# A two-layer graph network: the second layer's attention, stepped in two parts inside the graph loop, with its weights made ahead of the loop and its last part two tiles at a time

## The chip, the core and the metric

The kernel runs on one core of a Trainium2 chip, in float32. A core has a TensorE (PE; its weight loads are listed as PEld), a VectorE (DVE), a ScalarE (ACT), a GpSimd (POOL) and a SyncE (SP) that issues transfers. Each engine executes its own instructions in program order; semaphores make one wait for another. What counts is the device time of the whole kernel in microseconds (us); lower is better.

## What is computed

Two layers over 3125 nodes with 256 features. Each layer adds three things to `x`: a graph part over 50000 edges (sorted by target), an attention, and a network of experts. The change is in the second layer's graph part and attention, which both read the normalised `xn`:

```python
# graph part: 4 heads, messages of 64 features, softmax over the edges of a target
h_fwd, h_rev = h @ W_forward.T, h @ W_reverse.T
messages = h_fwd[src] * direction[:, 0:1] + h_rev[src] * direction[:, 1:2]
scores = leaky_relu(einsum('ef,hf->eh', messages, attn_forward[0]), 0.2)
exp_scores = exp(scores - scores.max(axis=0, keepdims=True))
norm = exp_scores / (segment_sum(exp_scores, dst)[dst] + 1e-10)
out = [segment_sum(messages * norm[:, hd:hd + 1], dst) for hd in range(4)]
# attention without a softmax: 8 heads of 64
q, k, v = split(einsum('bnc,fc->bnf', x, Wqkv))
k, v = _inst_norm_lastdim(k), _inst_norm_lastdim(v)   # over the 64 of a head
dots = einsum('bhnd,bhne->bhde', k, v)
out = einsum('bhnd,bhde->bhne', q, dots) / n
return einsum('bnf,cf->bnc', out, Wout) + bout
...
x = x + _L1_gnn_ref(xn, ...) + _L1_mix_ref(xn[None], ...)[0]
x = x + _L1_ffn_ref(_layernorm(x), ...)[0]
```

## The kernel before

`x` lies in SBUF as 25 tiles of 125 nodes. Layer 0 comes first, then `layer1_mix`, then `layer1_ffn`. In `layer1_mix`, `experts_in` ends layer 0, normalises `x`, keeps the transposed result `xT` and writes a table `tab1` of both products and their scores (136 values a node) to DRAM. Then the stage that is changed begins.

**The graph loop.** The 50000 edges are 391 columns of 128, taken in 49 groups of up to 8. For a group `i`:

- `fetch` issues 8 indirect gathers on POOL (the helper at L51), one for each column, into a buffer `g` of which there are four. It runs three groups ahead.
- `messages` (L1223 to L1234): three VectorE instructions make the messages and so free `g`; L1227 the scores, L1232 their maximum over the columns, and PE transposes it into `psm` (L1234).
- `maximum` (L1241 to L1247): VectorE takes the running maximum of each head, PE spreads it over the partitions by two more transposes (L1247).
- `ones_of` (L1272): a 0/1 matrix `hot` for each node tile that the group can touch, two of them mostly. Groups that touch a tile with all 8 columns alternate with groups that touch one with few.
- `exponents` (L1252 to L1257): scores less the maximum, then two exponentials on ScalarE.
- one group later `weigh` (L1280) multiplies messages by the four weights into `v`, and `products` (L1288) sums them into node tiles by matmuls of `hot` and `v`, in PSUM `pw`.
- two groups later `add` (L1297 to L1304) scales `acc` by what the maximum has grown and adds `pw`; a tile that is new is copied by ScalarE instead.

The order on PE, VectorE and ScalarE is the program's own here (`manual_schedule`): inside an iteration it is messages(i), weigh(i-1), maximum(i), products(i-1), add(i-2), ones and exponents(i). POOL and SP are ordered by the scheduler.

**The attention** is the generator `galerkin`, of which one step runs at the end of each iteration (`next(todo, None)`). Its first step loads the key and value weights in two transfers through one buffer `nat4` (L1507), transposes them on PE, copies them to `wkv` on ScalarE and takes the mean of each head's 64 columns off (L1517 to L1519). Then 26 steps: step `t` ends tile `t-1` (VectorE: variances L1528 to L1531, ScalarE: square root L1532, VectorE: reciprocal L1533 and the scaling of the keys L1534, PE: four matmuls into `pdots`, L1536) and begins tile `t` (four matmuls by the helper at L191, two copies L1546, squares L1548). Then one step that copies `dots`, loads and transposes `Wout`; one for `m2`, with the load of the query weights; and seven for the late part, a chunk of 3 or 4 tiles each: the first of these makes `g` (here the tile `gm`) too, and for each tile a product of `xT` and `gm` into PSUM, an add into `x` (L1585), and at the end of the chunk the bias (L1586). All 36 steps lie within the 51 iterations.

After the loop VectorE divides `acc` by the sums and adds it to `x`. `layer1_any_order` follows, which runs only for edges that are not in order: a branch (L1416) that all engines take, and then the expert network.

Of the kernel before, what the change touches and what calls it, by code (L numbers as in the profile page):

```python
# [8 lines left out]
F32 = mybir.dt.float32  # L9
# [3 lines left out]
OP = mybir.AluOpType  # L13
# [4 lines left out]
N = 3125  # L18
D = 256
P = 125  # L20
NT = 25
CHUNKS = ((0, 4), (4, 4), (8, 4), (12, 4), (16, 3), (19, 3), (22, 3))
# [66 lines left out]
class Kernel:  # L89
# [1082 lines left out]
    def layer1_mix(self):  # L1172
        nc, tc, a = self.nc, self.tc, self.a
        W, HD = 68, 64
        with ExitStack() as m:
# [130 lines left out]

            with tc.manual_schedule(engines={E_.PE, E_.DVE, E_.Activation}):
                todo = self.galerkin(big, wk, ps_a, ps_c, xT)
                starts = [(j0, min(GROUP, NJ - j0)) for j0 in range(0, NJ, GROUP)]
                G = len(starts)  # L1310
                ahead = [fetch(starts[i][0]) for i in range(3)]
                msg, exps, summed = {}, {}, {}
                for i in range(G + 2):
                    if i + 3 < G:
                        ahead.append(fetch(starts[i + 3][0]))
                    if i < G:
                        j0, n, g = ahead[i]
                        o, s, pt = messages(j0, n, g)
                    if 0 <= i - 1 < G:
                        weigh(starts[i - 1][1], msg[i - 1][0], exps[i - 1][2])  # L1320
                    if i < G:
                        pb = maximum(pt)
                    if 0 <= i - 1 < G:
                        summed[i - 1] = products(*starts[i - 1], exps[i - 1][2], msg[i - 1][1])
                    if 0 <= i - 2 < G:
                        add(*starts[i - 2], *exps[i - 2][:2], summed[i - 2])
                    if i < G:
                        msg[i] = o, ones_of(j0, n)
                        exps[i] = exponents(n, s, pb)
                    next(todo, None)  # L1330
                last = exps[G - 1][0]
# [167 lines left out]
    def galerkin(self, big, wk, ps_a, ps_c, xT):  # L1499

        nc, a = self.nc, self.a
        wkv = big.tile([128, 2, 1024], F32, name="wkv")
        for c4 in range(2):
            nat = wk.tile([128, 4, D], F32, name="nat4", bufs=1)
            nc.sync.dma_start(nat, a["L1_mix_Wqkv"][512 + 512 * c4:1024 + 512 * c4, :]  # L1507
                              .rearrange("(c p) d -> p c d", p=128))
            for k in range(2):
                pt = ps_a.tile([128, 4, 128], F32, name="ln_pt")  # L1510
                for i in range(4):
                    nc.tensor.transpose(pt[:, i, :], nat[:, i, k * 128:(k + 1) * 128], self.ident)
                nc.scalar.copy(wkv[:, k, 512 * c4:512 * c4 + 512],
                               pt.rearrange("p a b -> p (a b)"))
        heads = wkv.rearrange("p k (h c) -> p (k h) c", c=64)
        mean = big.tile([128, 32], F32, name="wkv_mean")
        nc.vector.tensor_reduce(mean, heads, AX.X, OP.add)  # L1517
# [1 line left out]
        nc.vector.tensor_sub(heads, heads, mean[:, :, None].to_broadcast([128, 32, 64]))  # L1519
        yield  # L1520

        pc = ps_c.tile([128, 4, 128], F32, name="pdots")
        kvs = {}
        for t in range(NT + 1):
            if t > 0:
                kv, sq = kvs.pop(t - 1)
                var = wk.tile([P, 16], F32, name="kv_var")
                nc.vector.tensor_reduce(var, sq, AX.X, OP.add)  # L1528
                nc.vector.tensor_scalar(var, var, 1.0 / 64, LN_EPS, op0=OP.mult, op1=OP.add)
                both = wk.tile([P, 8], F32, name="kv_both")  # L1530
                nc.vector.tensor_mul(both, var[:, 0:8], var[:, 8:16])  # L1531
                nc.scalar.activation(both, both, AF.Sqrt)  # L1532
                nc.vector.reciprocal(both, both)  # L1533
                nc.vector.tensor_mul(kv[:, 8:, :], kv[:, 8:, :], both[:, :, None].to_broadcast([P, 8, 64]))  # L1534
                for hp in range(4):
                    nc.tensor.matmul(pc[:, hp, :],  # L1536
                                     kv[:, 8 + 2 * hp:10 + 2 * hp, :].rearrange("p a b -> p (a b)"),
                                     kv[:, 2 * hp:2 * hp + 2, :].rearrange("p a b -> p (a b)"),
                                     start=(t == 1 and hp == 0), stop=(t == NT and hp == 3),
                                     skip_group_check=True)  # L1540
            if t < NT:
                kv = wk.tile([P, 16, 64], F32, name="kv")
                for i in range(2):
                    pk = ps_a.tile([P, 512], F32, name="ln_pt")
                    self.token_matmul(pk, xT, t, wkv[:, :, 512 * i:512 * i + 512])
                    nc.scalar.copy(kv[:, 8 * i:8 * i + 8, :].rearrange("p a b -> p (a b)"), pk)  # L1546
                sq = wk.tile([P, 16, 64], F32, name="kv_sq", bufs=1)
                nc.scalar.activation(sq, kv, AF.Square)  # L1548
                kvs[t] = kv, sq
            yield  # L1550
        dots = big.tile([128, 4, 128], F32, name="dots")
        nc.vector.memset(dots, 0.0)
        for s in (slice(0, 64), slice(64, 128)):
            nc.vector.tensor_copy(dots[s, :, s], pc[s, :, s])

        woT = big.tile([128, 4, D], F32, name="woT")
        nat = wk.tile([128, 2, 512], F32, name="nat4", bufs=1)
        nc.sync.dma_start(nat, a["L1_mix_Wout"].rearrange("(c p) f -> p c f", p=128))
        for cc in range(2):
            pt = ps_a.tile([128, 4, 128], F32, name="ln_pt")  # L1560
            for i in range(4):
                nc.tensor.transpose(pt[:, i, :], nat[:, cc, i * 128:(i + 1) * 128], self.ident)
            nc.scalar.copy(woT[:, :, cc * 128:(cc + 1) * 128], pt)
        yield
        m2 = big.tile([128, 4, D], F32, name="m2")
        for hp in range(4):
            pm = ps_a.tile([128, D], F32, name="ln_pt")
            nc.tensor.matmul(pm, dots[:, hp, :], woT[:, hp, :], start=True, stop=True)
            nc.vector.tensor_scalar(m2[:, hp, :], pm, 1.0 / N, None, op0=OP.mult)
        wq = wk.tile([128, 4, D], F32, name="nat4", bufs=1)  # L1570
        nc.sync.dma_start(wq, a["L1_mix_Wqkv"][0:512, :].rearrange("(c p) d -> p c d", p=128))
        yield
        g = big.tile([128, 2, D], F32, name="gm")
        for k in range(2):
            pm = ps_a.tile([128, D], F32, name="ln_pt")
            for hp in range(4):
                nc.tensor.matmul(pm, wq[:, hp, k * 128:(k + 1) * 128], m2[:, hp, :],
                                 start=(hp == 0), stop=(hp == 3))
            nc.scalar.copy(g[:, k, :], pm)
        bout = self.bcast(big, "L1_mix_bout")  # L1580
        for t0, n in CHUNKS:
            for t in range(t0, t0 + n):
                pm = ps_a.tile([P, D], F32, name="ln_pt")
                self.token_matmul(pm, xT, t, g)
                nc.vector.tensor_add(self.x[:, t, :], self.x[:, t, :], pm)  # L1585
            nc.vector.tensor_add(self.x[:, t0:t0 + n, :], self.x[:, t0:t0 + n, :],  # L1586
                                 bout[:, None, :].to_broadcast([P, n, D]))
            yield


# [393 lines left out]
```

## Time and profile before

| What | us |
|---|---|
| Kernel before, median of 3 runs | 2798.82 (2798.62 to 2800.9) |
| the profiled execution, its own time | 2800.13 |
| the profiled execution, span of its instructions | 2798.4 |
| PE busy in the span | 2201.9 |
| POOL busy | 1659.7 |
| DVE busy | 1508.4 |
| ACT busy | 544.0 |
| start of the first gather of `g` | 1613.86 |
| start of the last gather of `g` | 2223.53 |
| start of the last group's messages (L1223) | 2226.85 |
| first transfer in the chain of waits, behind the branch | 2269.77 |

All durations below are of the profiled execution. Times are from the start of its span. A line of the timeline has the start, the duration, the engine, the source line, the operation, the names of what it writes and reads, and, in brackets, how long the engine stood idle before it and who ended that. An engine that is busy for a large share of the whole need not be the one that sets the end of a given stage; that is read from the stage itself.

### The profile page before, as it was taken

The numbers are of one execution on the slowest core, as the hardware profiler recorded it, in microseconds if no ns is written. First come the engines' busy times: TensorE is split into PE (matmuls) and PEld (weight loads), VectorE is DVE, ScalarE is ACT, GpSimd is POOL, SyncE is SP. The second block draws the span as 40 slices with busy tenths as digits, with TensorE's granted clock in tenths as the row PEclk, the third lists the DMA queues.
The fourth block names the chain that finished last, engine by engine and source line by source line (L and its number), as shares of the span: only waits on it lengthen the run. The fifth ranks groups of instructions, "written<-read, shape, count | busy, mean of one in ns | idle before, by whom it ended". The sixth has DMA issues, their size and how long they took to land. (4 is left out here: it accounts for less than half of the span.)

```text
span 2798.4 us, 26658 instructions
## 1 busy us (share of the span) xinstructions
PE 2201.9 (79%) x9047; PEld 1657.6 (59%) x9047; DVE 1508.4 (54%) x3589; ACT 544.0 (19%) x1116; POOL 1659.7 (59%) x1486
## 2 busy tenths in 40 slices
PE   1761659999976997999999549998667756999963
PEld 1551547876763665888887436665555644666642
DVE  7976499455568701222111459988658861222226
ACT  2320000000011111222222424444000020132213
POOL 4888788773002804666665077777747606777751
PEclk9955769999977998999999669999888867999976
DMA  8920433224400304455553421111211121112252
GB/s 296 382 102 14 116 90 90 62 52 90 114 32 21 81 5 160 163 184 181 183 189 107 113 70 49 47 47 47 57 32 41 39 66 40 25 40 53 53 109 70
DMA packets 175937, 259.79 MB, mean 93 GB/s; under 512 B 53839, under 2 KB 140857, under 8 KB 172402
## 3 DMA queue, kind: packets, MB, share of 16 engines
q1 hardware_dynamic: 114273, 198.43, 23.1%
q0 software_dynamic: 52288, 47.17, 7.3%
q10 hardware_dynamic: 9222, 12.30, 1.4%
q8 instruction: 76, 1.25, 0.2%
q14 instruction: 78, 0.64, 0.1%
HBM read 173.99 MB, written 83.69 MB: 92 GB/s over the span
## 5 line engine op out<-in xcount | busy, mean ns | idle before, releaser
L58 POOL DMA_INDIRECT adj<-ch_sum,ch_place x391 | 505.9, 1294 | 152.8 <-issue 109.7
L51 POOL DMA_INDIRECT g<-tab,t_src x391 | 459.0, 1174 | 152.6 <-issue 110.8
L58 POOL DMA_INDIRECT sorted<-s_rows,pos x256 | 245.1, 957 | 181.9 <-DVE s_rows L1059 112.4
L460 PE MATMUL psum<-sup,adjT 125*125 125x256 f32 x1250 | 294.1, 395 | 50.9 <-DMA adjT<-adj 39.6
L1288 PE MATMUL pw<-v,hot 128*125 128x260 f32 x1244 | 318.1, 417 | 0.0
L51 POOL DMA_INDIRECT G<-tabg,g_src x256 | 252.6, 987 | 80.2 <-issue 71.2
L460 PEld LDWEIGHTS psum<-sup,adjT 125*125 125x125 f32 x1250 | 241.8, 195 | 92.7 <-DMA adjT<-adj 36.4
L1288 PEld LDWEIGHTS pw<-v,hot 128*125 128x125 f32 x1244 | 252.2, 206 | 47.0
L866 PE MATMUL ph<-xs,w 128*128 128x256 f32 x960 | 219.3, 387 | 22.9 <-issue 20.5
L866 PEld LDWEIGHTS ph<-xs,w 128*128 128x128 f32 x960 | 183.2, 193 | 58.2 <-issue 31.0
L894 PE MATMUL py<-w,h 128*128 128x256 f32 x960 | 216.7, 379 | 0.0
L1700 PE MATMUL fpy<-fw,fh 128*125 128x256 f32 x800 | 186.2, 389 | 32.9 <-DVE y L1702 28.0
L1700 PEld LDWEIGHTS fpy<-fw,fh 128*125 128x125 f32 x800 | 152.6, 192 | 70.4 <-DVE y L1702 29.2
L894 PEld LDWEIGHTS py<-w,h 128*128 128x128 f32 x960 | 180.1, 190 | 23.3
L868 ACT ACTIVATE h<-ph,b 128x256 f32<-128x256 f32 x240 | 113.4, 473 | 361.4 <-PE ph L866 330.1
L1692 PE MATMUL fph<-xT,fw 128*128 128x500 f32 (+1 forms) x448 | 175.8, 542 | 0.2 <-DMA fw<-in_L_ffn_W_dram 0.2
L1034 PE MATMUL pctx<-s_mv,s_ro 128*128 128x256 f32 x512 | 155.4, 415 | 1.9 <-DVE s_mv L1033 1.9
L58 POOL DMA_INDIRECT slots<-rows,abi x50 | 74.3, 1485 | 100.2 <-DVE r_cum L948 85.3
L897 DVE TENSOR_SCALAR yo<-py,own 128x256 f32<-128x256 f32 x60 | 27.8, 481 | 190.8 <-PE py L894 190.8
L1694 ACT ACTIVATE fh<-fph,cols 128x500 f32<-128x500 f32 (+1 forms) x112 | 70.2, 632 | 298.0 <-PE fph L1692 264.0
L1692 PEld LDWEIGHTS fph<-xT,fw 128*128 128x128 f32 x448 | 85.4, 192 | 72.0 <-issue 49.4
L463 DVE TENSOR_TENSOR x<-x,psum 125x512 f32<-125x512 f32 (+1 forms) x104 | 68.9, 664 | 109.4 <-PE psum L460 109.3
(535 smaller groups left out, 3355.0 us busy)
## 6 DMA issues: line engine op xcount, KB each, us to landing
adjT<-adj SPq DMA_DIRECT2D x25, 1367.2 KB
adj<-zero SPq DMA_DIRECT2D x22, 1536.0 KB
w<-in_L_ffn_W1p_dram SPq DMA_DIRECT2D x30, 1024.0 KB
w<-in_L_ffn_W2p_dram SPq DMA_DIRECT2D x30, 1024.0 KB
slots<-empty SPq DMA_DIRECT2D x1, 8448.0 KB
srow<-slots SPq DMA_DIRECT2D x30, 264.0 KB
adj<-ch_sum,ch_place POOLq DMA_INDIRECT x391
g<-tab,t_src POOLq DMA_INDIRECT x391
```

The lines of the kernel that those rows point to most:

```text
L51: nc.gpsimd.indirect_dma_start(out=out, out_offset=None, in_=table, in_offset=bass.IndirectOffsetOnAxis(ap=idx, axis=0))
L58: return nc.gpsimd.indirect_dma_start(out=table, out_offset=bass.IndirectOffsetOnAxis(ap=idx, axis=0), in_=rows, in_offset=None, **kw)
L460: nc.tensor.matmul(pm[:, i, :], mats[b][:, (a0 + i) * P:(a0 + i + 1) * P], sup[:, b, :], start=(b == b0), stop=(b == b0 + n - 1))
L463: nc.vector.tensor_add(xs, xs, pm[:, :m, :])
L866: nc.tensor.matmul(ph, w1[:, k, f * 128:(f + 1) * 128], xs[:, k, :], start=(k == 0), stop=(k == 1))
L868: nc.scalar.activation(h[:, f, :], ph, AF.Gelu, bias=b1[:, f:f + 1])
L894: nc.tensor.matmul(py, h[:, f, i * 128:(i + 1) * 128], w2[:, f, :], start=(f == 0), stop=(f == FC - 1))
L1034: nc.tensor.matmul(p1, ro[:, f - f0, :], mv, **st)
L1288: nc.tensor.matmul(pw.rearrange("p h c -> p (h c)"), hot[:, i - i0, :], v[:, i, :, :].rearrange("p h c -> p (h c)"), start=(i == i0), stop ...
L1692: nc.tensor.matmul(ph[:, :n * P], w1[:, k, f * 128:(f + 1) * 128], xT[:, k, t0 * P:(t0 + n) * P], start=(k == 0), stop=(k == 1))
L1694: nc.scalar.activation(hs[:, f, :n * P], ph[:, :n * P], AF.Gelu, bias=self.col("L1_ffn_b1", ei * FC + f))
L1700: nc.tensor.matmul(py, hs[:, f, i * P:(i + 1) * P], w2[:, f, :], start=(f == 0), stop=(f == FC - 1))
```

## The change

`galerkin` is stepped once ahead of the loop and then twice in each iteration: after `messages` and at the end.

- Its first part runs ahead of the loop: four buffers for four transfers on SP (key, value, output and query weights) and the bias's transfer behind them; the transposes for `wkv` and `woT`; `dots` is cleared; the bias is added to `x` in seven instructions; the mean is taken off `wkv`.
- Each attention step has two halves. In the first, after `messages`: variances and square root of tile `t-1`, matmuls, copies and squares of tile `t` (the squares' buffer is doubled). In the second, at the end: reciprocal, scaling of the keys and the matmuls into `pdots` of tile `t-1`. So the order in an iteration on VectorE is messages, variances, weigh, maximum, add, ones, exponents, scaling; and on PE the transpose of the maximum, the key-value matmuls, the two transposes back, products, `pdots`.
- `dots`, `m2` and `g` have steps of their own, with a step between a matmul and the use of its result; `m2` and `g` are made in PSUM tiles of two.
- The late part takes two tiles a group in 13 groups: matmuls of both tiles in the first half, one add of 125x512 in the second.

In the loop the steps now end in iteration 41 of 51.

```diff
                 todo = self.galerkin(big, wk, ps_a, ps_c, xT)
+                next(todo)
...
                         o, s, pt = messages(j0, n, g)
+                    next(todo, None)
                     if 0 <= i - 1 < G:
                         weigh(starts[i - 1][1], msg[i - 1][0], exps[i - 1][2])
...
         nc, a = self.nc, self.a
+        nats = []
+        for name, src in (("nat4", a["L1_mix_Wqkv"][512:1024, :].rearrange("(c p) d -> p c d", p=128)),
+                          ("nat4b", a["L1_mix_Wqkv"][1024:1536, :].rearrange("(c p) d -> p c d", p=128)),
+                          ("nat4c", a["L1_mix_Wout"].rearrange("(c p) f -> p c f", p=128)),
+                          ("nat4d", a["L1_mix_Wqkv"][0:512, :].rearrange("(c p) d -> p c d", p=128))):
+            nat = wk.tile([128, 2, 512] if name == "nat4c" else [128, 4, D], F32, name=name, bufs=1)
+            nc.sync.dma_start(nat, src)
+            nats.append(nat)
+        bout = self.bcast(big, "L1_mix_bout")
         wkv = big.tile([128, 2, 1024], F32, name="wkv")
         for c4 in range(2):
-            nat = wk.tile([128, 4, D], F32, name="nat4", bufs=1)
-            nc.sync.dma_start(nat, a["L1_mix_Wqkv"][512 + 512 * c4:1024 + 512 * c4, :]
-                              .rearrange("(c p) d -> p c d", p=128))
...
+        woT = big.tile([128, 4, D], F32, name="woT")
+        for cc in range(2):
...
+        dots = big.tile([128, 4, 128], F32, name="dots")
+        nc.vector.memset(dots, 0.0)
+        for t0, n in CHUNKS:
+            xs = self.x[:, t0:t0 + n, :]
+            nc.vector.tensor_add(xs, xs, bout[:, None, :].to_broadcast([P, n, D]))
...
         for t in range(NT + 1):
             if t > 0:
-                kv, sq = kvs.pop(t - 1)
+                old = kv
                 var = wk.tile([P, 16], F32, name="kv_var")
...
                 nc.scalar.activation(both, both, AF.Sqrt)
-                nc.vector.reciprocal(both, both)
-                nc.vector.tensor_mul(kv[:, 8:, :], kv[:, 8:, :], both[:, :, None].to_broadcast([P, 8, 64]))
-                for hp in range(4):
...
             if t < NT:
                 kv = wk.tile([P, 16, 64], F32, name="kv")
...
-                sq = wk.tile([P, 16, 64], F32, name="kv_sq", bufs=1)
+                sq = wk.tile([P, 16, 64], F32, name="kv_sq")
                 nc.scalar.activation(sq, kv, AF.Square)
-                kvs[t] = kv, sq
             yield
...
+            if t > 0:
+                nc.vector.reciprocal(both, both)
+                nc.vector.tensor_mul(old[:, 8:, :], old[:, 8:, :], both[:, :, None].to_broadcast([P, 8, 64]))
+                for hp in range(4):
...
+            yield
         for s in (slice(0, 64), slice(64, 128)):
             nc.vector.tensor_copy(dots[s, :, s], pc[s, :, s])
...
+        yield
         yield
         m2 = big.tile([128, 4, D], F32, name="m2")
-        for hp in range(4):
-            pm = ps_a.tile([128, D], F32, name="ln_pt")
-            nc.tensor.matmul(pm, dots[:, hp, :], woT[:, hp, :], start=True, stop=True)
-            nc.vector.tensor_scalar(m2[:, hp, :], pm, 1.0 / N, None, op0=OP.mult)
...
+        pms = []
+        for i in range(2):
+            pm = ps_a.tile([128, 2, D], F32, name="ln_pt")
+            for hp in range(2):
+                nc.tensor.matmul(pm[:, hp, :], dots[:, 2 * i + hp, :], woT[:, 2 * i + hp, :], start=True, stop=True)
+            pms.append(pm)
+        yield
+        for i, pm in enumerate(pms):
+            nc.vector.tensor_scalar(m2[:, 2 * i:2 * i + 2, :], pm, 1.0 / N, None, op0=OP.mult)
         yield
         g = big.tile([128, 2, D], F32, name="gm")
+        pm = ps_a.tile([128, 2, D], F32, name="ln_pt")
...
+        nc.scalar.copy(g, pm)
+        yield
+        yield
-        for t0, n in CHUNKS:
-            for t in range(t0, t0 + n):
-                pm = ps_a.tile([P, D], F32, name="ln_pt")
-                self.token_matmul(pm, xT, t, g)
-                nc.vector.tensor_add(self.x[:, t, :], self.x[:, t, :], pm)
-            nc.vector.tensor_add(self.x[:, t0:t0 + n, :], self.x[:, t0:t0 + n, :],
-                                 bout[:, None, :].to_broadcast([P, n, D]))
+        for t0 in range(0, NT, 2):
+            m = min(2, NT - t0)
+            pm = ps_a.tile([P, 2, D], F32, name="ln_pt")
+            for i in range(m):
+                self.token_matmul(pm[:, i, :], xT, t0 + i, g)
+            yield
+            xs = self.x[:, t0:t0 + m, :]
+            nc.vector.tensor_add(xs, xs, pm[:, :m, :])
             yield
```

## The prediction

> **What bounds the kernel now.** First the page's list of costliest groups: the gathers of layer 1's graph part (L51, `g`), 391 in number, take one engine from 1613.9 to 2224.7 us. Then the view of that tile alone, for its idle time:
>
> ```profile
> L51 POOL DMA_INDIRECT g<-tab,t_src x391 | 459.0, 1174 | 152.6 <-issue 110.8
> L51 POOL DMA_INDIRECT g<-tab,t_src x391: 940/947/2582, 1613.9 to 2223.5; - x196
> its engine sat idle before it (us, times) until:
>   issue: 112.1, 367
>   DVE score L1227: 35.1, 7
> ```
>
> Read: 459.0 busy + 152.6 idle = 611.6 us, all of the stage. A gather costs 0.945 us undisturbed and 0.306 us to the next: 391 x 1.25 = 488.8 us. What exceeds it is of two kinds: 459.0 - 391 x 0.944 = 89.9 us by which gathers were stretched, and 33 us (35.1 less 7 x 0.306) of waits for VectorE to free a buffer. Next the busy time by stretches (columns: length; PE, PEld, DVE, ACT, POOL busy with counts; PE clock; DMA), one each of phase A (groups 1 to 26, with the attention tiles), B (late part, groups 28 to 35) and C (graph groups alone):
>
> ```profile
> 1750.00:1800.00 50.00, 45.34 (x188) 30.98 (x187) 45.57 (x91) 23.68 (x39) 39.94 (x34) 1.00 0.18 48
> 2075.00:2100.00 25.00, 14.88 (x57) 11.63 (x55) 14.54 (x28) 0.78 (x4) 9.40 (x10) 0.86 0.11 29
> 2150.00:2200.00 50.00, 40.00 (x153) 31.17 (x153) 46.09 (x87) 3.32 (x18) 39.83 (x34) 0.86 0.18 48
> ```
>
> 34 gathers in 50 us and 34 x 0.306 between them: POOL is full in A and C. In B it isn't, and no other engine is either. The timeline there:
>
> ```profile
> 2093.43 2.75 PE L191 MATMUL ln_pt<-gm,xT 128*125 128x256 f32 x12
> ...
> 2094.50 0.42 DVE L1585 TENSOR_TENSOR x<-x,ln_pt 125x256 f32<-125x256 f32 x1 [7.14 <-PE ln_pt L191]
> ...
> 2097.55 0.72 DVE L1223 TENSOR_TENSOR msg<-g,t_dir 128x544 f32<-128x544 f32 x1
> ...
> 2099.93 0.94 POOL L51 DMA_INDIRECT g<-tab,t_src  x1 [7.65 <-DVE score L1227]
> ```
>
> The late matmuls stand behind the group's products on PE, VectorE's adds wait 7.14 us for them, the next group's messages stand behind the adds, and the gather waits for the buffer that they free. Starts of L1223 are 17 to 21 us apart in B, 11.5 to 12.5 in most of A. Five long POOL waits (6.8, 8.6, 5.8, 7.7, 5.6 us) make the 33 us; before them the surplus went into filling the four buffers, and in C VectorE (period 9.5) eats that stock and starts its last group 2.1 us after its gather ends. So the stage's end is POOL's end. The chain of waits starts only at 2269.8, behind the branch at L1416, so it doesn't show the stage; the branch and the expert network after it begin when the stage is done, and a shift of its end is a shift of the whole.
>
> Last, why gathers stretch, from the timeline of A:
>
> ```profile
> 1772.19 0.94 POOL L51 DMA_INDIRECT g<-tab,t_src  x1 [0.30 <-issue]
> 1772.21 2.30 DVE L1280 TENSOR_TENSOR v<-msg,v 128x2048 f32<-128x2048 f32 x1
> ...
> 1773.43 1.90 POOL L51 DMA_INDIRECT g<-tab,t_src  x1 [0.30 <-issue]
> ```
>
> The gather that starts 0.02 before the multiply runs as ever; the one that starts inside it ends at 1775.33, which is the multiply's end (1774.51) plus 0.82. The same holds for L1223 to L1225, L1272, L1297 and L1534; not for the reduce L1528.
>
> **What the Trainium skill says.** "SBUF — State Buffer", section "Who interferes with whom": VectorE's second SBUF port is GpSimd's, a VectorE instruction with two SBUF inputs contends with a GpSimd instruction that reads SBUF, `tensor_reduce` never does, and who issues first decides. The trace agrees (0.82 after the multiply; a gather inside L1528 stays at 0.94). "TensorE: Matmul & The Clock Gate", section "What's actually happening": the PE falls to half clock after an idle window of about 3.4 us. The trace agrees: clock 0.86 in B and C, 1.00 in most of A.
>
> **The change part by part.**
> 1. Late part. 7 steps of 3 or 4 tiles with adds behind their own matmuls become 13 steps of two: 8 matmul records (2.75/12 x 8 = 1.83 us of PE) between the maximum's two transposes, and one add of 125x512 from PSUM (about 0.66, from L463's row) at the end of the group. VectorE no longer waits on PE there: 8.7 busy (46.09 us over 5.3 groups) + 0.66 + about 0.5 of small waits = 9.9 us a group, under POOL's 11.75. The 33 us of POOL waits go. So do the waits for `m2` and `g`, now a half step apart.
> 2. Bias and weights ahead of the loop. Four loads of 512 KB and the bias go out on SP at about 1612.7; one load landed in 3.7 to 4.2 us, in 1614 to 1616 at 295 GB/s, so 2 MB take about 7 us more than latency: bias at about 1622. SP has nothing else queued until the branch. VectorE then does 7 bias adds (4 x 1.2 + 3 x 0.96 = 7.7), the mean (2.29) and the subtraction (2.29), and reaches group 0's messages at about 1635 instead of 1625.6. Nobody waits: the first gather that needs the buffer of group 0 is the 33rd, not before 1655. Groups 0 and 1 run late, with PE at half clock; VectorE catches up at about 1 us a group. The 7 adds leave B, where they cost nothing once POOL is the bound. Cost 0, at worst 2 us of stretched gathers.
> 3. Attention in two parts. VectorE's reduce and its two small ones (L1528, L1529, L1531) move ahead of the multiply L1280, the reciprocal and L1534 stay at the group's end; the waits for the square root (0.37) and for `psm` behind 3.6 us of key-value matmuls (0.1 to 0.9) go. VectorE's period falls from 11.9 to about 11.1 (busy 10.8). PE's 10.4 to 11.0 busy fits too. But POOL takes 10.0 plus the stretching, so what counts is where gathers now meet locks. I lay out one group from the start of its messages, as POOL would set it (the last gather ended 2.05 before): gathers start at -1.74, -0.49, 0.76 (in L1224 until 1.36: ends 2.18), 2.49, 3.74, 4.98. Before, L1280 stood at 2.50 to 4.79, and the gather at 3.74 lost 0.95. Now L1280 stands behind 1.6 us of L1528 to L1531, at 4.1 to 6.4, and the gather at 4.98 ends at 7.22: loss 1.30. The next start at 7.53 is free, the one at 8.78 falls into L1272, which begins at 8.6 where two tiles are added (k=8: ends 9.79) and at 7.8 where one is: it ends at 10.6, or about 10.1 to 10.4; losses 0.89 or 0.3 to 0.6. With 0.42 at L1224 the sum is 2.6 or about 2.15, mean 2.35 a group: a group of 12.35 us. In A before, groups 0 to 26 took 1613.9 to 1934.4.
>
> **The sum.** Groups 0 to 2: 35 us. Groups 3 to 26: 24 x 12.35 = 296. Groups 27 to 48 (21.9 of them): 11.75 each as C ran before (the same sum for C: 10.0 + 0.42 + 0.95 + 0 to 0.9) = 257. Together 588: the gathers end at 1613.9 + 588 = 2202 instead of 2224.7. Gain 22.7 us, which is the 33 us of waits less about 10 given back in A. In the profiled execution (span 2798.4, its own time 2800.1) that makes 2777.4; it lies 1.3 above the median, so for the median of 2798.8 I say 2776.
>
> **Unknown sizes.** The stretching: not below 74 us over all groups (1.5 each: only L1224's 0.42 and a multiply's least loss of 0.95, and little more), not above 115 (2.35 everywhere). Gathers then end between 2177 and 2218 if POOL never waits: gains of 48 to 7. PE's clock in A: above, a cold key-value step (5.29 instead of 3.60, as at 1918.9) delays the maximum by 1.7, which VectorE's 1.9 us of L1272 covers; below, nothing to gain.
>
> **The rivals.**
> - Forecast, POOL full and A's groups at about 12.35: 2766 to 2788. Chance 0.57.
> - R1, same cause, but the stretching stays at the 1.83 a group of the trace before (89.9/49): 488.8 + 92 = 581, end 2195, gain 30 to 40: 2758 to 2768. For it: it was 1.93 in A and 1.75 in C whatever VectorE's period was. Against: there VectorE's order was another. Chance 0.22.
> - R2, a new wait in A or B takes most of it: PE runs late because pairs of products (up to 6.84) and key-value matmuls now share a group with a maximum between, or the clock falls; half of the gain goes: 2788 to 2796. Against it: 0.8 to 1 us of room on each engine. Chance 0.10.
> - R3, slower: the moved multiply. If gathers fall so that L1280 catches one at its start (loss 2.1 instead of 1.30) and both L1272 hit, A's group is 13.3 or more. It decides from 11.9 + 33/24 = 13.3 us a group on; at 13.8 it costs 24 x 1.9 - 33 = +12: 2811. For it: in L1280's old place a gather started 0.02 before it, a margin that no longer protects. Against: gathers are set in step by L1224, and 4.98 lies 0.9 inside. Chance 0.08, with 0.03 left for what I don't see.
>
> A change under 0.2% (5.6 us) can't be told from none here. Range 2758 to 2795: R1 and most of R2 are inside. Faster 0.87, same 0.05, slower 0.08.
>
> **What would show it.** Right: `g` has no wait for score L1227 over 1 us; L1585's idle before it is gone; the last gather starts at about 2201; starts of L1223 12.2 to 12.6 apart in A and about 11.75 after it; the gather inside L1280 about 2.25 us long. Step 2 is wrong if a gather waits before 1670. Step 3 is wrong if gathers in A lose under 2.0 a group (R1) or over 3.3 (R3). The forecast as a whole is wrong if VectorE is found to wait for PE rather than for gathers in A.

## The result, and the profile after

| | before | after |
|---|---|---|
| median of 4 runs each, us | 2798.72 | 2764.81 |
| lowest and highest, us | 2790.55, 2800.9 | 2761.53, 2766.42 |
| profiled execution: own time and span, us | 2800.1, 2798.4 | 2766.24, 2764.5 |
| first gather starts, last gather ends, us | 1613.86, 2224.73 | 1612.23, 2190.74 |
| gathers: beyond 391 x 0.944, us | 89.9 | 90.5 |
| gathers: waits beyond the usual 0.306, us | 33.0 | 0 |
| from the last gather's end to the end of the span, us | 573.7 | 573.8 |

The ratio is 0.988, 95% interval [0.9863, 0.9898]: 33.9 us faster, where 22.7 were forecast and the rival R1 gave 30 to 40. The median lies in R1's range (2758 to 2768), 1.2 us below the forecast's own (2766 to 2788). The last row says that nothing after the stage gave back or added anything. So the difference lies in the stage, which is 32.4 us shorter (610.9 to 578.5 us from the first gather's start to the last one's end), and in a first gather that started 1.6 us earlier. Among the runs below that start varies by more (1604.4 to 1612.3, where the kernel before takes about 2799 us).

The row of the gathers in the page's list of costliest groups, then the view of that tile (first line: shortest, median and longest duration in ns, first and last start; "issue" is idle time for which the profile shows no wait):

```profile
L51 POOL DMA_INDIRECT g<-tab,t_src x391 | 459.6, 1175 | 119.7 <-issue 106.8
```

```profile
L51 POOL DMA_INDIRECT g<-tab,t_src x391: 940/945/2762, 1612.2 to 2189.5; - x196
its engine sat idle before it (us, times) until:
  issue: 106.8, 351
  DMA g<-tab,t_src: 73.2, 64
...
who waited for it (us, times):
  DVE msg L1223: 67.8, 46
```

Busy time didn't move (459.0 to 459.6). The idle time fell from 152.6 to 119.7, which is 391 x 0.306: the row "DVE score L1227: 35.1, 7" of the view before has no successor. The row of 73.2 us "until DMA" is mostly not POOL's: the view counts every instruction that touches `g`, and 67.8 us of it is VectorE's L1223. The last two lines name it: VectorE now waits for gathers in 46 of 49 groups, 67.8 us. The view before had, in the same place:

```profile
who waited for it (us, times):
  DVE msg L1223: 15.7, 9
```

The order of who waits for whom has turned round.

The same three phases by stretches (columns as in the prediction: length; PE, PEld, DVE, ACT, POOL busy with counts; PE clock; DMA share and GB/s); the last one is shortened to the stage's end:

```profile
1750.00:1800.00 50.00, 46.70 (x189) 31.38 (x187) 46.42 (x89) 22.81 (x38) 39.64 (x35) 1.00 0.19 49
2075.00:2100.00 25.00, 18.87 (x80) 14.67 (x79) 19.85 (x39) 1.48 (x8) 19.82 (x18) 0.93 0.19 49
2150.00:2187.00 37.00, 26.73 (x92) 20.05 (x90) 27.77 (x51) 1.89 (x10) 29.08 (x27) 0.82 0.19 49
```

In the second line POOL has 18 gathers in 25 us where it had 10, and is as full as in the other two. A group of the late part, from the timeline:

```profile
2046.71 2.30 DVE L1280 TENSOR_TENSOR v<-msg,v 128x2048 f32<-128x2048 f32 x1
...
2047.05 1.89 PE L191 MATMUL ln_pt<-gm,xT 128*125 128x256 f32 x8
2047.93 1.89 POOL L51 DMA_INDIRECT g<-tab,t_src  x1 [0.30 <-issue]
...
2053.35 0.68 DVE L1602 TENSOR_TENSOR x<-x,ln_pt 125x512 f32<-125x512 f32 x1
...
2055.99 0.72 DVE L1223 TENSOR_TENSOR msg<-g,t_dir 128x544 f32<-128x544 f32 x1 [1.96 <-DMA g<-tab,t_src]
```

The matmuls of two tiles run while VectorE multiplies; the add (now L1602) has no idle time before it, where its forerunner waited 7.14 us for PE; and the next group's messages wait 1.96 us, for the gather.

### The profile page after: what moved, and what is told of

Its sections match the earlier page's. It is cut to its first block, busy times and chain, and to the rows that moved or that the text cites. A ratio compares the mean times of both kernels' runs of the same rounds, so it can differ in the third digit from the quotient of the medians.

```text
span 2764.5 us, 26618 instructions
## 1 busy us (share of the span) xinstructions
PE 2192.9 (79%) x9047; PEld 1649.0 (60%) x9047; DVE 1502.0 (54%) x3575; ACT 545.3 (20%) x1115; POOL 1660.4 (60%) x1486
## 5 line engine op out<-in xcount | busy, mean ns | idle before, releaser
L51 POOL DMA_INDIRECT g<-tab,t_src x391 | 459.6, 1175 | 119.7 <-issue 106.8
L1288 PE MATMUL pw<-v,hot 128*125 128x260 f32 x1244 | 306.9, 407 | 0.0
L51 POOL DMA_INDIRECT G<-tabg,g_src x256 | 253.7, 991 | 80.2 <-issue 71.5
L1288 PEld LDWEIGHTS pw<-v,hot 128*125 128x125 f32 x1244 | 244.4, 200 | 43.6
```

The costliest lines, as they stand in the source:

```text
L51: nc.gpsimd.indirect_dma_start(out=out, out_offset=None, in_=table, in_offset=bass.IndirectOffsetOnAxis(ap=idx, axis=0))
L1288: nc.tensor.matmul(pw.rearrange("p h c -> p (h c)"), hot[:, i - i0, :], v[:, i, :, :].rearrange("p h c -> p (h c)"), start=(i == i0), stop ...
```

## The experiments

T1 is the theory that the gain is the late part's POOL waits and nothing else, and that what remains of the stage is gathers held by VectorE's two-input instructions. T2, its rival, is that the gain comes from the shorter attention step or the weights' place. A third question is the moved multiply: is a held gather what a group costs, and would R3's shift have made the kernel slower?

The twelve runs were on several chips. On two of them the whole kernel takes longer (before: 3194.53 and 3176.41 us), and why isn't known. Most of the excess lies outside the stage: in all but one of the profiles from there the first gather starts at 1857 to 1864 us and 692 to 704 us follow the last one, where the others have 573 to 576, and the stage of one and the same kernel (the late part alone) took 586.3 us there and 583.9 elsewhere. So times are compared as ratios to the kernel before on the same chip, and stages by their own length.

**The late part put back.** The changed kernel with the old late part:

```diff
-        for t0 in range(0, NT, 2):
-            m = min(2, NT - t0)
-            pm = ps_a.tile([P, 2, D], F32, name="ln_pt")
-            for i in range(m):
-                self.token_matmul(pm[:, i, :], xT, t0 + i, g)
+        yield
+        for t0, n in CHUNKS:
+            for t in range(t0, t0 + n):
+                pm = ps_a.tile([P, D], F32, name="ln_pt")
+                self.token_matmul(pm, xT, t, g)
+                nc.vector.tensor_add(self.x[:, t, :], self.x[:, t, :], pm)
             yield
-            xs = self.x[:, t0:t0 + m, :]
-            nc.vector.tensor_add(xs, xs, pm[:, :m, :])
             yield
```

> The changed kernel with the late part as before: chunks of 3 or 4 tiles at the end of a group, adds behind their own matmuls (the bias stays ahead of the loop). Theory T1 (POOL's gathers set the stage; the gain is the 33 us that they waited for VectorE in the late part): those waits come back, the time is 2798 +- 6 us, and the groups with late chunks are 17 to 20 us apart. Theory T2 (the gain is VectorE's shorter period in the attention groups, whose two waits are gone): no more than a third is lost, 2775 us or less.

Measured: 3182.04 beside 3194.53, ratio 0.9958 [0.9943, 0.9972]; the profiled execution took 3251.6 us, so its trace says little. A second run of the same kernel:

> The same kernel as e1_old_late (late part in chunks, adds behind their own matmuls) once more, since its profile was disturbed by stretches of 10 to 20 us in which PE stood still. T1: the five POOL waits of 5 to 9 us for score L1227 are back, the stage is as long as before within 8 us, the time is 2 +- 6 us below the kernel before. T2 (the gain is VectorE's shorter period in the attention groups): at least 22 below.

3168.02 beside 3176.41, ratio 0.9971 [0.9952, 0.9989]. The view of the gathers' tile in this run:

```profile
L51 POOL DMA_INDIRECT g<-tab,t_src x391: 939/944/2760, 1856.7 to 2468.7; - x196
...
its engine sat idle before it (us, times) until:
...
  DVE score L1227: 34.1, 5
```

The wait for L1227 is back with five times and 34.1 us (32.6 beyond 0.306 each), the stage takes 613.2 us, as long as before (610.9) within 3, and most of the gain is gone, with the weights still ahead and the attention still in two parts. What is left is 8.4 us (0.29%; 0.42% in the first run), a little more than T1's 2 +- 6 and far from the 22 of T2, which falls as the main cause.

**The late part alone.** The kernel before with only the late part exchanged: its loop over pairs of tiles, the steps of their own for `m2` and `g`, and the second step in each iteration. Attention stays in one piece at the group's end, the weights in the loop, and so does the bias, in seven groups ahead of the late part (an excerpt of the edit):

```diff
                         o, s, pt = messages(j0, n, g)
+                    next(todo, None)
...
+        for t0 in range(0, NT, 2):
+            m = min(2, NT - t0)
+            pm = ps_a.tile([P, 2, D], F32, name="ln_pt")
+            for i in range(m):
+                self.token_matmul(pm[:, i, :], xT, t0 + i, g)
+            yield
+            xs = self.x[:, t0:t0 + m, :]
+            nc.vector.tensor_add(xs, xs, pm[:, :m, :])
             yield
```

> The kernel before with the new late part alone (two tiles a group in two halves, the halves of m2 and gm apart; the attention steps in one piece at the group's end and the weights in the first iteration as before; the bias in seven groups ahead of the late part). T1: no gather waits over 1 us for a buffer, attention groups stay at 11.9 apart as before, 2766 +- 6 us. T2: the attention groups keep their waits, so at least 10 us of the gain are missing: 2776 us or more.

3148.16 beside 3194.53, ratio 0.9852 [0.9813, 0.9892]; no wait of POOL over 1 us. Later once more, on a chip where before took 2797.64:

> The kernel before with the new late part alone, once more, beside the next run. T1 (the gain is the late part's POOL waits, and attention in two parts is worth nothing while POOL sets the groups): within 5 us of the changed kernel, a ratio of 0.986 to 0.990 to the kernel before. Rival (attention in two parts brings something of its own): 8 us or more short of the changed kernel, ratio 0.991 or above.

2770.54, ratio 0.9904 [0.9884, 0.9923], that is 27 us. The number lies in the gap between the two expectations (0.990 and 0.991). The stage took 583.9 us here and 578.5 in the changed kernel; whether these 5 us belong to the attention in two parts is read from the gathers' own times:

| gathers, us | before | changed | late part alone |
|---|---|---|---|
| groups 0 to 26 | 320.5 | 324.8 | 320.4 |
| groups 27 to 48 | 290.3 | 253.7 | 263.4 |

They don't. Through group 26 the kernel with attention in one piece is the faster one, by 4.4 us (in the earlier run of this kernel 321.1; in the two runs above and below with attention in two parts 326.1 and 326.6). What it lacks comes after it, and 6.8 of the 9.7 us there are in the seven groups that hold the bias's adds. One of them:

```profile
2009.86 1.24 DVE L1595 TENSOR_TENSOR x<-x,b_L_mix_bout 125x1024 f32<-125x1024 f32 x1
...
2011.02 2.28 DVE L1280 TENSOR_TENSOR v<-msg,v 128x2048 f32<-128x2048 f32 x1
2011.09 3.03 POOL L51 DMA_INDIRECT g<-tab,t_src  x1 [0.30 <-issue]
```

The add stands ahead of the multiply and shifts it, so that a gather starts 0.07 us inside it and takes 3.03 us. So the late part carries 27 of the 34 us. By these traces attention in two parts and the weights ahead cost 4 us up to group 26, and the late groups without the bias's adds bring back 9.7; in the time of the whole kernel the remainder isn't shown, since the intervals of the two ratios overlap (the changed kernel's goes up to 0.9898).

**The weights back in the loop.** The changed kernel with the first part of `galerkin` in the first iteration instead of ahead of the loop:

```diff
                 todo = self.galerkin(big, wk, ps_a, ps_c, xT)
-                next(todo)
...
-                    next(todo, None)
+                    if i > 0:
+                        next(todo, None)
```

> The changed kernel with the first part of the attention (weights, bias adds, mean) in the first iteration instead of ahead of the loop. T1: the gathers have three groups of stock then and wait for nobody, 2765 +- 4 us. Rival: the weights ahead of the loop save VectorE's 7.75 us wait for them, so that 5 to 8 us come back: 2770 to 2773 us.

3146.35 beside 3194.53, ratio 0.9842 [0.9807, 0.9878]: all of the gain is there without it, no POOL wait, a stage of 581.9 (groups 0 to 2 took 37.5 us instead of 35.1). The place of this part, ahead of the loop or in its first iteration, is worth nothing that the time shows. The bias's adds are in the first iteration here, so this run doesn't say what they would cost in the late part.

**The multiply back in its old place.** The first half of the attention step behind L1280 instead of ahead of it, so that VectorE multiplies where it did before the change:

```diff
-                    next(todo, None)
                     if 0 <= i - 1 < G:
                         weigh(starts[i - 1][1], msg[i - 1][0], exps[i - 1][2])
+                    next(todo, None)
```

> The changed kernel with the first half of the attention step behind the multiply of messages and weights instead of ahead of it, so that the multiply stands at 2.5 to 4.8 us of a group in all phases. T1 with the laid-out group: the gather at 3.73 loses 0.95 instead of 1.23, the later ones meet L1272 less (one at 8.42 starts just ahead of it or loses 0.3): attention groups 11.3 to 11.6 apart instead of 12.06 on the mean, 2757 +- 5 us. Rival (the stretch is the same wherever the multiply stands, as the sum before and after suggests): 2765 +- 4 us.

3155.03 beside 3194.53, ratio 0.9865 [0.9827, 0.9902], in a profile in which PE stood still for 20.5 us in the middle of the stage and POOL had three waits of 17 us together. Once more, on a chip where before took 2799.17:

> The same kernel as e5_weigh_first (first half of the attention step behind the multiply L1280) once more, since in that profile PE stood still for 20 us and more at a few places with nothing to wait for, so that its sum says little. T1 with the laid-out group: gathers lose 0.95 at L1280 instead of 1.23, attention groups 11.3 to 11.7 apart where nothing stands still, 34 + 8 = 42 +- 5 us below the kernel before. Rival (the stretch is the same wherever the multiply stands): 34 +- 3 below.

2761.8, ratio 0.9876 [0.9855, 0.9897]: 37.4 us, where the two expectations meet (37 to 47 and 31 to 37), so the time doesn't decide. The trace shows the layout: the gather 3.73 us after the messages' start took 1.89 us (a loss of 0.95, as the prediction laid out for the old place), groups stood 11.3 to 11.65 apart in mid phase A, and the stage was 4.0 us shorter than the changed kernel's. Two groups near the end of phase A lost it again (13.4 and 13.6). The profiled execution as a whole was 11 us shorter than the changed kernel's, but 8 of them lie ahead of the stage.

**The multiply cut up.** If gathers are held to the end of the instruction they started in, shorter instructions must hold them less, with the same elements multiplied. The changed kernel with L1280 in two and in four instructions (below: four; two has steps of 4 columns):

```diff
-                nc.vector.tensor_mul(v[:, :n, :, :HD], o[:, :n, None, :HD].to_broadcast([128, n, 4, HD]),
-                                     v[:, :n, :, HD:].to_broadcast([128, n, 4, HD]))
+                for a0 in range(0, n, 2):
+                    a1 = min(n, a0 + 2)
+                    nc.vector.tensor_mul(v[:, a0:a1, :, :HD], o[:, a0:a1, None, :HD].to_broadcast([128, a1 - a0, 4, HD]),
+                                         v[:, a0:a1, :, HD:].to_broadcast([128, a1 - a0, 4, HD]))
```

> The changed kernel with the multiply L1280 in two instructions of 4 columns each (about 1.2 us each). T1 (a gather that starts inside a VectorE instruction with two SBUF inputs waits for its end): in attention groups the gather at 4.98 starts inside the first half (4.05 to 5.25) and loses about 0.15 instead of 1.23, the next one starts at about 6.38, at the second half's end; groups fall to VectorE's own 11.1 to 11.5. In the graph groups after it the gather at 3.73 falls into the second half (3.66 to 4.85) and loses 0.95 as before. 34 + 12 = 46 +- 5 us below the kernel before. Rival (gathers are slowed by VectorE's SBUF traffic as such, so cutting the instruction changes nothing): 34 - 3 = 31 +- 3 below.

> The changed kernel with L1280 in four instructions of 2 columns (about 0.63 us each). T1: no gather can lose more than 0.5 at it; attention groups 11.1 to 11.5 apart as VectorE needs (three instructions more, 0.2 us), graph groups 11.0 instead of 11.55; 34 + 12 + 22 x 0.5 = 57 +- 7 us below the kernel before, the sum of the stretching under 70 us (90.5 now). Rival: no shorter stretching, 34 - 5 = 29 below.

Beside 2799.17 before: two instructions 2753.4, ratio 0.9841 [0.9822, 0.9861]; four 2732.2, ratio 0.9759 [0.974, 0.9778]: 45.8 us below before, as T1 had it, and 67.0, 3 more than the top of its range. The stretching went from 90.5 to 81.0 and 58.1 us, the stage from 578.5 to 569.0 and 546.2. The row of the gathers with four, and one of its graph groups from the timeline:

```profile
L51 POOL DMA_INDIRECT g<-tab,t_src x391 | 427.2, 1093 | 119.7 <-issue 108.4
```

```profile
2033.59 0.95 POOL L51 DMA_INDIRECT g<-tab,t_src  x1 [0.30 <-issue]
2033.61 2.55 DVE L1282 TENSOR_TENSOR v<-msg,v 128x512 f32<-128x512 f32 x4
...
2034.84 0.94 POOL L51 DMA_INDIRECT g<-tab,t_src  x1 [0.30 <-issue]
```

The four pieces take 2.55 us together, 0.25 more than one instruction, yet the gather that starts in their midst, at 2034.84, where the second piece gives way to the third, runs its plain 0.94 us; beside the one long instruction it took 1.89 (2047.93 above). Thirty gathers that start inside a piece are still held, but none takes more than 1.37 us. Put down to the instruction in which each gather starts, the loss at the multiply fell from 53.9 to 5.4 us over the stage, and about 16 us came back at others that gathers now meet more often, L1223 and L1272 above all. No kernel run here was faster than this one.

**The multiply moved to a gather's start.** R3 said that the multiply could catch a gather at its start. L1280 is moved ahead of the group's small reduce L1232; it begins 2.26 us after the messages' start, instead of 4.05 in attention groups and 2.50 in graph groups. Nothing is added or left out:

```diff
-            def messages(j0, n, g):
+            def messages(j0, n, g, between):
...
+                between()
                 mx = gp.tile([128, 4], F32, name="mx1")
...
+                    def last_weights():
+                        if 0 <= i - 1 < G:
+                            weigh(starts[i - 1][1], msg[i - 1][0], exps[i - 1][2])
+
                     if i < G:
                         j0, n, g = ahead[i]
-                        o, s, pt = messages(j0, n, g)
+                        o, s, pt = messages(j0, n, g, last_weights)
+                    else:
+                        last_weights()
                     next(todo, None)
-                    if 0 <= i - 1 < G:
-                        weigh(starts[i - 1][1], msg[i - 1][0], exps[i - 1][2])
```

> The changed kernel with the multiply L1280 moved ahead of the maximum's reduce (L1232), so that it starts at about 2.27 us of a group instead of 4.05 in the attention groups and 2.50 in the others; nothing is added or left out. T1: the gather that starts at 2.48, 0.02 ahead of the multiply in the graph groups so far, now starts inside it and ends 0.82 behind its end (4.57), 2.9 us long, a loss of 1.97 instead of 1.23 or 0.95; graph groups 12.5 to 12.7 apart instead of 11.55, attention groups about 12.6 instead of 12.06; together about 35 us more than the changed kernel, as slow as the kernel before within 10 us. Rival (a place 0.2 us earlier can't matter where VectorE has a microsecond of slack): 34 +- 4 us below the kernel before, like the changed kernel.

3189.55 beside 3176.41, ratio 1.0028 [1.0009, 1.0048]: slower than before, with the late part's gain inside. The gathers' row and a graph group of this run:

```profile
L51 POOL DMA_INDIRECT g<-tab,t_src x391 | 512.0, 1309 | 119.7 <-issue 116.6
```

```profile
2262.24 2.28 DVE L1281 TENSOR_TENSOR v<-msg,v 128x2048 f32<-128x2048 f32 x1
2262.46 2.88 POOL L51 DMA_INDIRECT g<-tab,t_src  x1 [0.30 <-issue]
```

The gather starts 0.22 us after the multiply instead of 0.02 before it, and takes 2.88 us: until 2265.34, the multiply's end (2264.52) plus 0.82. Groups stood 12.7 apart in phase A and 13.06 in C, the stretching was 142.9 us, the stage 630.9 where the changed kernel had 578.5. There is no wait of POOL in it (idle 119.7 as ever): the 52 us are stretching alone. T1 had 35: that is what gathers lose more at the multiply (89.8 us instead of 53.9); 10 more are lost at L1272, which other gathers now meet. The rival, that 0.2 us can't matter, falls.

**One input instead of two.** Is it the two inputs or the length that holds gathers? L1280 as a product of the messages with the constant 1.0, so that the weights of the four heads are left out:

```diff
-                nc.vector.tensor_mul(v[:, :n, :, :HD], o[:, :n, None, :HD].to_broadcast([128, n, 4, HD]),
-                                     v[:, :n, :, HD:].to_broadcast([128, n, 4, HD]))
+                nc.vector.tensor_scalar(v[:, :n, :, :HD], o[:, :n, None, :HD].to_broadcast([128, n, 4, HD]),
+                                        1.0, None, op0=OP.mult)
```

> The changed kernel with L1280 as a multiply of the messages by the constant 1 (one SBUF input instead of two; the weights of the four heads are left out of the messages, so the result is another). T1 (two SBUF inputs hold the port): if the instruction keeps its length of about 2.3 us, gathers that start inside it run 0.95 us as elsewhere, the stretching falls by about 50 us to 40, and the stage ends about 35 us earlier than in the changed kernel. Rival (any VectorE instruction of that length delays a gather, whatever its inputs): the gather inside it stays at 2.2 us.

2757.72 in its one run, beside 2799.17. Neither expectation holds as written, since the instruction didn't keep its length: 1.22 us for the same 2048 elements. The Trainium skill, "VectorE: DVE Perf Modes", section "What auto-detection actually checks", states that an instruction can run in a mode of twice the rate if its single source and its destination are in SBUF; 1.22 us instead of 2.29 agrees. It did hold gathers, in another manner, as the timeline of a graph group shows:

```profile
2027.13 1.38 POOL L51 DMA_INDIRECT g<-tab,t_src  x1 [0.30 <-issue]
2027.15 1.24 DVE L1280 TENSOR_SCALAR v<-msg 128x2048 f32<-128x2048 f32 x1
```

A gather that starts 0.02 us ahead runs its plain 0.94 us beside the two-input multiply; here it is held until 2028.51, which is the instruction's end (2028.39) plus 0.12. The same holds for all 43 gathers that had started up to 0.33 us ahead. A hold to an end plus some 0.115 us is what the Trainium skill states for a transfer beside a VectorE copy, "SBUF — State Buffer", section "A bandwidth-pool intuition that's wrong (but worth ruling out)"; the 0.12 agrees. The four gathers that started inside the one-input product ended 0.82 us after it, as they do with two inputs, so 0.12 or 0.82 is a matter of when the gather starts. The stretching stayed at 82.6 us.

So this run doesn't separate inputs from length. The trace of the kernel before does, with two instructions of one shape and length that stand close behind each other, a sum with one input and a subtraction with two:

```profile
1638.54 2.29 DVE L1517 TENSOR_REDUCE wkv_mean<-wkv 128x32 f32<-128x2048 f32 x1 [7.75 <-ACT wkv L1513]
1639.11 0.94 POOL L51 DMA_INDIRECT g<-tab,t_src  x1 [0.30 <-issue]
...
1641.08 2.29 DVE L1519 TENSOR_TENSOR wkv<-wkv,wkv_mean 128x2048 f32<-128x2048 f32 x1
1641.60 2.58 POOL L51 DMA_INDIRECT g<-tab,t_src  x1 [0.30 <-issue]
```

Both gathers start half a microsecond inside; the first runs as ever, the second is held to the end plus 0.81. So length alone doesn't hold a gather. Nor is a second input needed, as the product with 1.0 shows: of the one-input instructions the reduces don't hold, and that product does.

**Cut up, with the attention in one piece.** Is the shorter attention step worth something once the multiply holds nothing up? The kernel of "the late part alone" with L1280 in four:

> The same kernel, attention in one piece, with L1280 as four instructions of two columns. T1: with the locks gone VectorE's own period sets phase A (11.9 as before plus 0.2 for the three more instructions, against the 11.3 of e7_split_four), so that this run ends 24 x 0.6 to 0.8 = 14 to 19 us behind e7_split_four: a ratio of 0.981 to 0.983 to the kernel before; the gathers are as little stretched as there (60 us or less). Rival (attention's place is worth nothing here either): as e7_split_four, 0.976.

2734.37, ratio 0.9776 [0.9756, 0.9795], which can't be told from 0.9759 [0.974, 0.9778] for four instructions with attention in two parts. T1's 14 to 19 us fell. The tile's view says why:

```profile
L51 POOL DMA_INDIRECT g<-tab,t_src x391: 939/947/2422, 1608.0 to 2154.5; - x196
...
its engine sat idle before it (us, times) until:
...
  DVE score L1227: 9.0, 7
```

VectorE's groups in phase A were 12.2 us apart (11.3 in the other), as expected, but POOL didn't stand still for it: it filled the buffers ahead, waited for L1227 for 7 us more than usual in three groups (9.0 less 7 x 0.306), and in the rest of the stage VectorE caught up at 9.87 us a group. Against these 7 us stand 5.5 us less of stretching (52.6 instead of 58.1). The stage took 547.5 us, against 546.2.

## Why the prediction was right, and which term was off

- What bounds: right. The stage's end is POOL's end. The last gather of the profiled execution ended 34.0 us earlier, the medians differ by 33.9, and the 573.7 us behind it became 573.8.
- Step 1, the late part: right in kind and size. All five waits went, 33.0 us, and they came back when the late part was put back. No new wait took their place (R2).
- Step 2, the weights and the bias: priced at 0, at worst 2 us of stretched gathers. Groups 0 to 2 took 35.1 us (35 in the sum) where they had taken 33.2, and the first messages started at 1635.0, as laid out; no gather waited before 1670. One reason in it was wrong: that the bias's adds cost nothing in the late part once POOL is the bound. In the late part alone, where they stayed, they shift the multiply onto a gather's start. The first gather of all came 1.6 us earlier, which the sum didn't have.
- Step 3, attention in two parts: the step whose size was off. It was to give back about 10 us in phase A; through group 26 the changed kernel gave back 4.3 (324.8 us instead of 320.5). The table has the sum's terms beside what the trace has, from first to last gather:

| term | predicted, us | measured, us |
|---|---|---|
| first gather starts at | 1613.9 | 1612.2 |
| groups 0 to 2 | 35 | 35.1 |
| groups 3 to 26 | 296 (12.35 each) | 289.7 (12.07 each) |
| groups 27 to 48 | 257 (11.75 each) | 253.7 |
| gathers end at | 2202 | 2190.7 |

Of the 11.2 us by which the sum was too long, 6.3 lie in groups 3 to 26, 3.3 in the later ones and 1.6 in the first gather's start. The laid-out group had two losses of weight. The one at L1280 came out as drawn: the gather at 4.98 ended 7.16 us after the messages' start (7.22), a loss of 1.23 (1.30). The one at L1272 did not. Both in one attention group of the changed kernel, whose messages start at 1770.30:

```profile
1774.36 2.29 DVE L1280 TENSOR_TENSOR v<-msg,v 128x2048 f32<-128x2048 f32 x1
...
1775.28 2.18 POOL L51 DMA_INDIRECT g<-tab,t_src  x1 [0.30 <-issue]
...
1778.71 1.66 DVE L1272 SCALAR_TENSOR_TENSOR hot<-t_dst,node 128x375 f32<-128x375 f32 x2
1779.01 1.06 POOL L51 DMA_INDIRECT g<-tab,t_src  x1 [0.30 <-issue]
```

L1272's two instructions come here with the shorter (0.54 us) ahead, and the gather falls into the short one: it took 1.06 us, a loss of 0.11 where 0.89 were in the sum. In the next group, with one add, L1272 ended 0.1 us after the gather's start and cost next to nothing, where 0.3 to 0.6 were in the sum. The prediction had taken the long one as first in every group with two adds. In groups 18 to 27 the losses came about as priced: two groups at 12.63 and 12.35 us had gathers of 1.91 and 1.71 us in L1272. Mean length of a group: 11.6 us in groups 5 to 17, 12.3 from 18 on; the stretching about 1.7 and 2.3 a group, where 2.35 was taken for all. The mean of groups 3 to 26 is 2.08, just above the 2.0 below which R1 was to hold. So the whole came out at 90.5 us, R1's number, though not for R1's reason, that the stretching stays what it is: it rose from 3.1 to 5.0 us in groups 0 to 2 and from 47.6 to 50.0 in groups 3 to 26, and fell from 39.2 to 35.6 in the rest. In groups 3 to 26 the multiply took 32.2 instead of 26.0 us of it and L1224 7.2 instead of 0.8, while the scaling of the keys (L1534) took 0.5 instead of 7.1 and L1272 8.9 instead of 10.6. That these make up almost the old total is luck, and R1's number owes its fit to it. (R1's own sum has 92 us where 49 x 1.83 makes 89.9; with it the stage is 578.7 us, and 578.5 were measured.) The late groups, 3.3 us cheaper than taken, were mostly 11.3 and 11.7 to 11.8 us in turn rather than 11.75 each.

The waits that step 3 was to take from VectorE did go. In groups 3 to 26 VectorE had waited 11.6 us for PE and 8.7 us for ScalarE; now it waits for neither there, but 19.6 us for gathers.

- R3 was given 0.08 and didn't come in this kernel, but its mechanism is real: with the multiply begun 2.26 us after the messages' start the stage is 52 us longer. Its place was drawn too narrow: attention groups then took 12.7 us, under the 13.3 from which it was to decide, and it was the graph groups, at 13.06, that made the rest.
- The clock: the prediction takes PE's 0.86 in B and C as the mark of idle windows of about 3.4 us. In C the trace doesn't show that: between 2150 and 2200 us PE was never idle for more than 2.2 us at a stretch, and its clock still stood at half for 3.4 and 6.8 us at a time. Nothing in the sum rests on it.

Left open: why groups 18 to 27 fall into another pattern than 5 to 17, what the attention in two parts is worth with the bias left where it is now (no run has that alone), and what makes the kernel longer on two of the chips.

## What to carry to other kernels

When one engine's stream sets a stage, add up its idle time by releaser and its busy time beyond the undisturbed duration: the first sum is what a reordering of another engine can free, and here, where the stage ended with that stream, it came through whole. A shorter period of an engine that had slack, or that could catch up later through buffers, was worth nothing here, though it was visible in every group. Where a stream of gathers runs beside VectorE, keep two-input instructions short: cutting one of 2.3 us into four cost VectorE 0.25 us and won 32 us of stretching here, and moving one ahead of a single small reduce lost 52. Adds of 1.0 to 1.2 us put ahead of it cost about 7 us in seven groups. So look at which instruction each gather starts in before moving anything.

## What was not expected of the hardware

- It is the moment of the gather's start that counts. One that starts 0.02 us before the two-input multiply of 2.3 us runs 0.94 us beside it; one that starts 0.22 us after its beginning takes 2.88, until 0.82 us after its end. The multiply itself stayed at 2.28 to 2.30 in both cases.
- The one-input product of the same 2048 elements took 1.22 us instead of 2.29, and it holds a gather that is already under way (by up to 0.33 us), until 0.12 us after its end; one that starts inside it ends 0.82 us after, as with two inputs.
- A one-input reduce of 2.29 us over the same 128x2048 elements holds no gather: 0.94 us.
- POOL and VectorE lock in step: eight gathers and a group of VectorE settle into a pattern in which the same gather meets the same instruction for ten groups and more (groups 5 to 17 here, all 11.5 to 12.0 us long), so that a loss recurs in group after group.
